# Two token blocks per gate/up chain in a fused state-space and int4 feed-forward kernel

## The chip, the cores and the metric

The kernel runs on one core of a Trainium2 chip. The metric is the device time of one launch in microseconds (us), as the median of several runs. Engines are named as in the profile: PE multiplies matrices, PEld loads its weights, DVE is the vector engine, ACT the scalar (activation) engine, POOL the general-purpose engine, and SP issues most of the DMA transfers.

## The reference: what is computed

The input x has 32 sequences of 64 heads, each of length 1024. Each head is convolved over its length with a state-space kernel K, the product is cut to the sequence's own length, and a feed-forward network with 4-bit weights follows over the 1024 features. Cut to what matters:

```
dtA = A * exp(log_dt);  P = dtA * arange(1024)
K   = 2 * Re( sum_n C * (exp(dtA) - 1) / A * exp(P) )          # one kernel per head
y   = causal_convolution(u * mask, K) + u * mask * D;  y = y * mask
W   = q * s[group] - (z[group] + 1) * s[group]                 # groups of 128 rows
gate, up = y @ Wg, y @ Wu                                      # 1024 -> 2752
out = x + float16( (gate * sigmoid(gate) * up) @ Wd )          # 2752 -> 1024
```

A token is a pair of head and sequence, so there are 64 x 32 = 2048 tokens.

## The kernel before

**Tokens.** The tokens are cut into four blocks of 512, of 16 heads each. For each block the kernel convolves, then computes gate and up, then the down product, and adds the result to x. The convolution's output is held as the sum of two f16 tensors, `xh` and `xl` (tile `self.x`, two buffers of one block each), so every product with it is two matmuls.

**Convolution.** `group` makes the kernels of four or eight heads (phase tables L344-349 with help of DVE or POOL, factors on DVE, a small matmul `kq` L328) and stores them to a DRAM tensor `kpad`. `toeplitz` (L402-410) reads 512 KB of it per head in such a way that the tile holds the Toeplitz matrix. For the first block most of these matrices go into the tiles that later hold the gate and up weights (`w`); the others go into three buffers `t0`. `conv_head` (L413-448) runs 24 matmuls per head (L430) on the input split into `uh` and `ul`; after two heads DVE masks the sum into `y` (L442), ACT casts it to `xh` (L444), and POOL (DVE for the last pair of the first block) subtracts to get `xl` (L446). Matrices are asked for up to four heads ahead.

**Weights.** `unpack` (L454-478) turns 128 x 512 words of 4-bit values into fp8 on DVE: two splits (L466, L467) and eight additions of the zero points (L474). The result goes to a DRAM tensor `m` and is read back in the right layout (L485). Ten such chunks make gate and up, six make the down weights. The loads, stores and reloads are issued by SP, in order with all other SP transfers.

**Chains.** Scales differ per group of 128 rows. Instead of scaling the weights, a chain multiplies its accumulator in PSUM after each group by the ratio of two scales. `gu_chain(ct, blk)` (L513-546) makes one tile of 128 of the 5504 gate and up columns for one block: 8 groups, each two matmuls 128x512 (L520, L521) into one PSUM bank and, but for the last, one rescale of 128x512. There are 43 tiles; gate tile i (Silu into `sg`, L528) is followed by up tile i, whose product with `sg` is `v` (DVE, L534), split into `ih` (ACT cast, L535) and `il` (POOL, L244); the 43rd tile is half gate, half up. `dn_chain(nt, blk)` (L549-568) makes one of eight output tiles: 21 groups of two matmuls (L555, L556) and a rescale, a last matmul (L560), a scaled copy `o` (ACT, L566), the addition to x (L567) and the store.

**Order.** `rescale` (L505-511) gives each rescale to DVE (L508) or ACT (L511) by a running balance, `lag`, of assumed nanoseconds. `roll` (L578-613) interleaves up to six chains (four in the last down stage), one step of each in turn, and advances side work by rates: unpacking and, during the first block's chains, the kernels of heads 16 to 31 and the second convolution; during block 1's, the kernels of heads 32 to 63 and the third convolution; during block 2's, the fourth. Only the first convolution stands ahead of the first chains, with a few unpacking steps between its matmuls. A scheduler then orders each engine's instructions with these as priorities. PSUM has eight banks: six for chains (`ps_ch`), two for convolutions and kernel products (`ps_cv`).

Of the kernel before, what the change touches and what calls it, by code (L numbers as in the profile page):

```python
# [9 lines left out]
F32 = mybir.dt.float32  # L10
# [20 lines left out]
UNPACK_RATE, CONV1_RATE = 0.25, 0.4  # L31
GU_SIDE_RATES, DN_SIDE_RATE = {1: 0.2, 2: 0.15}, 1.0
CHAIN_LEAD = 1.34
# [182 lines left out]
class Core:  # L216
    def __init__(self, ctx, tc, io):
# [8 lines left out]
        self.ps_ch = pool("ps_ch", bufs=6, space=PSUM)  # L226
        self.ps_cv = pool("ps_cv", bufs=2, space=PSUM)
# [4 lines left out]
        self.sg, self.t0, self.us = {}, {}, {}  # L232
# [5 lines left out]
        self.ih = keep.tile([128, 21, 512], F16, name="ih")  # L238
        self.il = keep.tile([128, 21, 512], F16, name="il")
        self.ic = keep.tile([128, 512], F16, name="ic")  # L240
# [11 lines left out]
    def scratch(self, tiles):  # L252
        spaces = [[t.rearrange("p g t -> p (g t)"), 0] for t in tiles]

        def take(shape, dt, name=None):
            n = 1
            for d in shape[1:]:
                n *= d
            size = n * SIZE[dt] // 2
            for sp in spaces:  # L260
                if sp[1] + size <= sp[0].shape[1]:
                    v = sp[0][:shape[0], sp[1]:sp[1] + size].bitcast(dt)
                    sp[1] += size
                    if len(shape) == 3:
                        v = v.rearrange("p (a b) -> p a b", b=shape[2])
                    return v
            raise ValueError(name)

        return take
# [52 lines left out]
    def make_kernel(self, pool, e1, e2, h0, nh):  # L322
        nc = self.nc
        bank = dict(pool=self.ps_ch, tag="ch") if h0 < 16 else dict(pool=self.ps_cv, tag="cv")
        q = bank["pool"].tile([32, 8, 32], F32, name="kq", tag=bank["tag"])[:, :nh, :]
# [7 lines left out]
        for k in range(2):  # L333
            nc.sync.dma_start(self.kpad[h0:h0 + nh, k, 128:].rearrange("h (a b) -> a h b", b=32), kb[:, k])
# [8 lines left out]
    def group(self, pool, h0, nh, xd, tables=None):  # L343
        nc, co = self.nc, self.co  # L344
        side = nc.vector if h0 < 16 else nc.gpsimd
        self.taps(pool, h0)
        with self.after({16: ("y", 4), 24: ("y", 7)}.get(h0)):
            s1, s2, sq_op = phase_tables(nc, side, tables or pool, co, self.cst, h0, nh)
        self.mark(f"sq{h0}", sq_op)
        self.dve(2000)  # L350
# [3 lines left out]
        self.dve(1000)  # L354
# [5 lines left out]
    def groups(self, pool, starts):  # L360
        if len(starts) == 4:
            steps = decay_tables_wide(self.nc, pool, self.co, self.cst, starts[0], 32)
            next(steps)
            for _ in range(4):
                yield
            with self.after("act"):
                xds = next(steps)
        else:
            with self.after("sq8"):
                xds = [decay_tables(self.nc, pool, self.co, self.cst, h0) for h0 in starts]  # L370
# [5 lines left out]
    def conv_fetch(self, h0):  # L376
        src = self.io["xF"][:, h0:h0 + 4, :].rearrange("(c p) h b -> p c h b", p=128)
        cut = lambda d: self.take([128, 8, 4 * B], d).rearrange("p c (h b) -> p c h b", b=B)
        u, uh, ul = cut(F32), cut(F16), cut(F16)
        self.nc.sync.dma_start(u, src)  # L380
        return u, uh, ul

    def conv_split(self, u, uh, ul):
        with self.after("sq4"):
            self.nc.scalar.copy(uh, u)
        with self.after(("e", 4)):
            self.nc.vector.tensor_tensor(ul, u, uh, ALU.subtract)
        return uh, ul
# [13 lines left out]
    def toeplitz(self, h):  # L402
        if h < 8 or 11 <= h < 16:
            j = h if h < 8 else h - 9
# [8 lines left out]
    def conv_head(self, hh):  # L413
        nc = self.nc
        h = hh % 16
        for k in (hh, hh + 1):
            if k // 4 not in self.us and k // 16 == hh // 16:
                self.us[k // 4] = self.conv_load(4 * (k // 4))
        for k in range(hh, hh + (5 if hh < 16 else 3)):
            if k not in self.t0 and k // 16 == hh // 16 and k in self.known:  # L420
# [3 lines left out]
        if h % 2 == 0:  # L424
            bank, tag = (self.ps_ch, "ch") if hh < 16 else (self.ps_cv, "cv")
            self.cq = bank.tile([128, 8, 2, B], F32, name="cq", tag=tag)
        q = self.cq
# [8 lines left out]
        if h % 2 == 1:  # L436
            ts = slice(32 * (h - 1), 32 * (h + 1))
            y = self.ys.pop(0) if hh < 16 else self.cv.tile([128, 8, 2, B], F32, name="y", bufs=1)
            yv = y.rearrange("p g h b -> p g (h b)")
            xh, xl = self.x[hh // 16 % 2]  # L440
            with self.tc.high_priority(offset=100), nullcontext():
                self.mark(("y", hh // 2), nc.vector.tensor_tensor(  # L442
                    y, q, self.mask.unsqueeze(2).to_broadcast([128, 8, 2, B]), ALU.mult))
                nc.scalar.copy(xh[:, :, ts], yv)  # L444
                split = nc.vector if hh == 15 else nc.gpsimd
# [8 lines left out]
    def unpack(self, src, zsrc, dst, rows, w):  # L454
# [7 lines left out]
        a = up.tile([128, 2, 512], I32, name="upk_a")[:rows, :, :w]  # L462
# [42 lines left out]
    def rescale(self, q, col):  # L505
        if self.lag <= 0:
            self.dve(660)
            self.nc.vector.tensor_scalar(q, q, col, None, ALU.mult)  # L508
        else:
            self.act(580)  # L510
            self.mark("act", self.nc.scalar.activation(q, q, AF.Copy, scale=col))  # L511

    def gu_chain(self, ct, blk):  # L513
        nc = self.nc
        q = self.ps_ch.tile([128, 512], F32, name="chq", tag="ch")
        xh, xl = self.x[blk % 2]
        cols = slice(128 * (ct % 21 % 4), 128 * (ct % 21 % 4) + 128)
        for g in range(GH):
            lw = self.wmix[:, g] if ct == 42 else self.wgu[ct // 21][ct % 21 // 4][:, g, cols]
            nc.tensor.matmul(q, lw, xh[:, g, :], start=(g == 0), stop=False, skip_group_check=True)  # L520
            nc.tensor.matmul(q, lw, xl[:, g, :], start=False, stop=(g == GH - 1), skip_group_check=True)  # L521
            if g < GH - 1:
                self.rescale(q, self.rgu[:, ct, g:g + 1])
                yield
        last = self.lgu[:, ct:ct + 1]
        if ct < 21:
            sg = self.fw.tile([128, 512], F32, name="sg", tag="sg", bufs=3)
            nc.scalar.activation(sg, q, AF.Silu, scale=last)  # L528
            self.act(580)
            self.sg[ct] = sg  # L530
        elif ct < 42:
            i = ct - 21
            v = self.fw.tile([128, 512], F32, name="v", bufs=2)
            nc.vector.scalar_tensor_tensor(v, q, last, self.sg.pop(i), ALU.mult, ALU.mult)  # L534
            nc.scalar.copy(self.ih[:, i, :], v)  # L535
            self.dve(660)
            self.act(520)
            self.pool_first(self.il[:, i, :], v, self.ih[:, i, :], ALU.subtract)
        else:
            sg = self.fw.tile([128, 512], F32, name="sg", tag="sg", bufs=3)  # L540
            v = self.fw.tile([128, 512], F32, name="v", bufs=2)
            a, b = slice(0, 64), slice(64, 128)
            nc.scalar.activation(sg[b], q[a], AF.Silu, scale=last[a])
            nc.vector.scalar_tensor_tensor(v[b], q[b], last[b], sg[b], ALU.mult, ALU.mult)
            nc.scalar.copy(self.ic[b], v[b])
            nc.vector.tensor_tensor(self.ic[a], v[b], self.ic[b], ALU.subtract)
        yield

    def dn_chain(self, nt, blk):  # L549
        nc = self.nc  # L550
        q = self.ps_ch.tile([128, 512], F32, name="chq", tag="ch")
        for g in range(GI):
            lw = self.wd[g // 8][nt // 4][:, g % 8, 128 * (nt % 4):128 * (nt % 4) + 128]
            if g < 21:
                nc.tensor.matmul(q, lw, self.ih[:, g, :], start=(g == 0), stop=False, skip_group_check=True)  # L555
                nc.tensor.matmul(q, lw, self.il[:, g, :], start=False, stop=False, skip_group_check=True)  # L556
                self.rescale(q, self.rdn[:, nt, g:g + 1])
                yield
            else:
                nc.tensor.matmul(q, lw, self.ic, start=False, stop=True, skip_group_check=True)  # L560
        rows, cols = slice(128 * nt, 128 * nt + 128), slice(512 * blk, 512 * blk + 512)
# [218 lines left out]
```

## Time and profile before

| What | Value |
|---|---|
| median of 3 runs | 1089.41 us (1087.74 to 1090.03) |
| profiled execution, own time | 1086.84 us |
| its span on the core | 1085.1 us |
| granted PE clock | 0.991 |
| PE, PEld busy | 1024.5, 513.5 us |
| DVE, ACT busy | 905.2, 831.9 us |
| POOL busy | 224.3 us |
| DMA moved | 82.28 MB |

The profile is of one execution, and its span leaves out what lies before the first and after the last instruction. Busy time of an engine includes overlapping instructions only once; a mean duration of one instruction may include overlap with the next. In rows of windows the columns are the window, its length and PE, PEld, DVE, ACT, POOL with busy time and number of instructions, then the granted clock, the DMA share and GB/s. In rows of groups the last part says how long the engine was idle ahead of them and what ended it; rows of waits give the total, the number and the longest.

### The profile page before, as it was taken

The numbers are of one execution on the slowest core, as the hardware profiler recorded it, in microseconds if no ns is written. First come the engines' busy times: TensorE is split into PE (matmuls) and PEld (weight loads), VectorE is DVE, ScalarE is ACT, GpSimd is POOL, SyncE is SP. The second block draws the span as 40 slices with busy tenths as digits, with TensorE's granted clock in tenths as the row PEclk, the third lists the DMA queues.
The fourth block names the chain that finished last, engine by engine and source line by source line (L and its number), as shares of the span: only waits on it lengthen the run. The fifth ranks groups of instructions, "written<-read, shape, count | busy, mean of one in ns | idle before, by whom it ended". The sixth has DMA issues, their size and how long they took to land.

```text
span 1085.1 us, 15582 instructions
## 1 busy us (share of the span) xinstructions
PE 1024.5 (94%) x5834; PEld 513.5 (47%) x5834; DVE 905.2 (83%) x1458; ACT 831.9 (77%) x1371; POOL 224.3 (21%) x178
## 2 busy tenths in 40 slices
PE   2877988899999999999999999999999999999997
PEld 2743444455344445444564444444564444444443
DVE  8989999977998898777768778787768888887887
ACT  5337978877788997777768777777768888888876
POOL 0312234231502121121223012131212111111000
PEclk9899999999999999999999999999999999999999
DMA  5963666530102030110343010011321000000011
GB/s 139 295 222 117 214 188 188 156 123 7 49 1 88 11 92 20 35 44 20 131 132 127 11 49 21 21 56 61 127 79 67 31 30 1 1 1 1 1 40 39
DMA packets 78389, 82.28 MB, mean 76 GB/s; under 512 B 16902, under 2 KB 49798, under 8 KB 78314
## 3 DMA queue, kind: packets, MB, share of 16 engines
q1 hardware_dynamic: 78314, 81.30, 23.4%
q8 instruction: 45, 0.74, 0.3%
q14 instruction: 30, 0.25, 0.1%
HBM read 64.15 MB, written 17.14 MB: 75 GB/s over the span
## 4 chain that ended last, share of the span: by engine, by line
PE 80%; DVE 11%; ACT 3%; DMA 3%; issue 2%; POOL 1%; SPq 0%; DVEq 0%; ACTq 0%; POOLq 0%
PE chq L520 24%; PE chq L521 23%; PE chq L555 13%; PE chq L556 13%; PE cq L430 6%; DVE upk_m L474 3%; DVE chq L508 2%; ACT chq L511 2%; DMA m<-upk_m 1%; DVE v L534 1%; PE chq L560 1%; DMA w<-kpad 1%; PE kq L328 1%; DMA t<-kpad 0%; POOL il L244 0%
## 5 line engine op out<-in xcount | busy, mean ns | idle before, releaser
L520 PE MATMUL chq<-xh,w 128*128 128x512 f16 x1344 | 505.3, 379 | 15.9 <-DVE chq L508 8.2
L511 ACT ACTIVATE chq<-chq,gur 128x512 f32<-128x512 f32 x678 | 431.5, 666 | 98.7 <-PE chq L521 90.6
L521 PE MATMUL chq<-xl,w 128*128 128x512 f16 x1344 | 504.2, 379 | 0.0
L508 DVE TENSOR_SCALAR chq<-chq,gur 128x512 f32<-128x512 f32 x526 | 391.6, 755 | 79.9 <-PE chq L521 58.0
L508 DVE TENSOR_SCALAR chq<-chq,dnr 128x512 f32<-128x512 f32 x321 | 238.6, 755 | 61.5 <-PE chq L556 50.1
L511 ACT ACTIVATE chq<-chq,dnr 128x512 f32<-128x512 f32 x351 | 228.1, 661 | 73.0 <-PE chq L556 68.4
L555 PE MATMUL chq<-ih,wd 128*128 128x512 f16 x672 | 253.0, 379 | 3.0 <-DVE chq L508 1.7
L556 PE MATMUL chq<-il,wd 128*128 128x512 f16 x672 | 253.1, 379 | 0.0
L521 PEld LDWEIGHTS <-w 128*128 128x128 fp8e4 x1344 | 131.2, 98 | 158.4 <-issue 30.5
L244 POOL TENSOR_TENSOR il<-v,ih 128x512 f16<-128x512 f32 x84 | 105.9, 1261 | 461.3 <-ACT ih L535 461.3
L520 PEld LDWEIGHTS <-w 128*128 128x128 fp8e4 x1344 | 131.1, 98 | 135.3 <-issue 2.8
L430 PEld LDWEIGHTS <-t 128*128 128x128 f16 x1224 | 103.0, 98 | 95.5 <-issue 4.0
L430 PE MATMUL cq<-uh,t 128*128 128x256 f16 (+7 forms) x768 | 134.6, 226 | 1.2 <-DMA t<-kpad 1.2
L474 DVE TENSOR_TENSOR upk_m<-upk_a,upk_z 128x512 fp8e4<-128x512 uint8 (+2 forms) x144 | 100.3, 738 | 1.0 <-DMA m<-upk_m 1.0
L556 PEld LDWEIGHTS <-wd 128*128 128x128 fp8e4 x672 | 65.6, 98 | 64.7 <-issue 6.3
L555 PEld LDWEIGHTS <-wd 128*128 128x128 fp8e4 x672 | 65.6, 98 | 61.1 <-issue 1.6
L430 PE MATMUL cq<-ul,t 128*128 128x256 f16 (+7 forms) x384 | 86.3, 225 | 3.5 <-POOL ul L244 3.5
L534 DVE SCALAR_TENSOR_TENSOR v<-chq,gul,sg 128x512 f32<-128x512 f32 x84 | 62.6, 746 | 21.9 <-ACT sg L528 11.6
L528 ACT ACTIVATE sg<-chq,gul 128x512 f32<-128x512 f32 x84 | 57.8, 688 | 11.1 <-PE chq L521 10.3
L535 ACT CAST ih<-v 128x512 f16<-128x512 f32 x84 | 51.6, 614 | 14.6 <-DVE v L534 14.5
L446 POOL TENSOR_TENSOR xl<-y,xh 128x512 f16<-128x512 f32 x24 | 30.3, 1262 | 103.3 <-ACT xh L444 86.0
L567 POOL TENSOR_TENSOR xr<-xr,o 128x512 f32<-128x512 f32 x24 | 28.2, 1177 | 85.8 <-ACT o L566 72.8
(177 smaller groups left out, 448.4 us busy)
## 6 DMA issues: line engine op xcount, KB each, us to landing
t<-kpad SPq DMA_DIRECT2D x51, 512.0 KB, 3.5
w<-kpad SPq DMA_DIRECT2D x13, 512.0 KB, 6.4
u<-xF SPq DMA_DIRECT2D x12, 512.0 KB, 4.1
xr<-xT SPq DMA_DIRECT2D x24, 256.0 KB, 3.5
out<-xr SPq DMA_DIRECT2D x24, 256.0 KB, 2.3
m<-upk_m SPq DMA_DIRECT2D x10, 512.0 KB, 4.4
w<-m SPq DMA_DIRECT2D x10, 512.0 KB, 4.2
upk_p<-qgu SPq DMA_DIRECT2D x10, 256.0 KB, 6.4
```

The lines of the kernel that those rows point to most:

```text
L244: self.nc.gpsimd.tensor_tensor(out, a, b, op)
L430: nc.tensor.matmul(q[:, d:, h % 2, :], t0[:, lw, 128 * d:128 * d + 128], uu[:, 0:8 - d, h % 4, :], start=(d == 0 and k == 0 and h % 2 == 0 ...
L474: nc.vector.tensor_tensor(out, q, minus, ALU.add, saturate=False)
L508: self.nc.vector.tensor_scalar(q, q, col, None, ALU.mult)
L511: self.mark("act", self.nc.scalar.activation(q, q, AF.Copy, scale=col))
L520: nc.tensor.matmul(q, lw, xh[:, g, :], start=(g == 0), stop=False, skip_group_check=True)
L521: nc.tensor.matmul(q, lw, xl[:, g, :], start=False, stop=(g == GH - 1), skip_group_check=True)
L528: nc.scalar.activation(sg, q, AF.Silu, scale=last)
L534: nc.vector.scalar_tensor_tensor(v, q, last, self.sg.pop(i), ALU.mult, ALU.mult)
L535: nc.scalar.copy(self.ih[:, i, :], v)
L555: nc.tensor.matmul(q, lw, self.ih[:, g, :], start=(g == 0), stop=False, skip_group_check=True)
L556: nc.tensor.matmul(q, lw, self.il[:, g, :], start=False, stop=False, skip_group_check=True)
```

## The change

`gu_chain(ct)` now makes one tile for two token blocks at once. Its accumulator has two PSUM banks; per group there are four matmuls, and one rescale of 128x1024 covers both banks. `sg` and `v` are 1024 wide. The products of the first block stay in `ihl` (which replaces `ih` and `il`); those of the second go through a tile `spill` to DRAM and are read back into `ihl` step by step while the last down chain of the first block runs. `dn_chain(n0, blk)` holds two output tiles in two banks, with rescales of 128x512 as before, and stores 512 KB at once.

There are six stages: gate/up of blocks 0 and 1; down 0; down 1; gate/up of blocks 2 and 3; down 2; down 3. Four chains run at once (three in the first two down stages). Convolutions 0 and 1 both stand ahead of the first chains, with the kernels of heads 8 to 31, unpacking and scale ratios at set places between their matmuls; all their matrices use the weight tiles and three `t0` buffers in turn, and are asked for eight heads ahead. Kernels of heads 32 to 63 and convolutions 2 and 3 run beside the two first down stages. One POOL step of the kernel tables of heads 16 to 31 moves to DVE, the kernel stores of heads 0 to 7 move to ACT's DMA queue, the unpacking scratch `upk_a` has one buffer instead of two, and `y` has two instead of one. All PSUM tiles come from one pool of four two-bank buffers.

```diff
-UNPACK_RATE, CONV1_RATE = 0.25, 0.4
-GU_SIDE_RATES, DN_SIDE_RATE = {1: 0.2, 2: 0.15}, 1.0
-CHAIN_LEAD = 1.34
+UNPACK_RATE, LATE_RATE = 0.3, 1.8
+CHAIN_LEAD = 2.0
...
-        self.ps_ch = pool("ps_ch", bufs=6, space=PSUM)
-        self.ps_cv = pool("ps_cv", bufs=2, space=PSUM)
+        self.ps = pool("ps", bufs=4, space=PSUM)
...
+        self.ihl = keep.tile([128, 21, 2, 512], F16, name="ihl")
+        self.ic = [keep.tile([128, 512], F16, name=f"ic{b}") for b in range(2)]
+        self.spill = self.dram.tile([21, 128, 2, 512], F16, name="spill")
+
+    def psum(self, name):
+        return self.ps.tile([128, 2, 512], F32, name=name, tag="ch")
...
-            nc.sync.dma_start(self.kpad[h0:h0 + nh, k, 128:].rearrange("h (a b) -> a h b", b=32), kb[:, k])
+            (nc.scalar if h0 < 8 else nc.sync).dma_start(
+                self.kpad[h0:h0 + nh, k, 128:].rearrange("h (a b) -> a h b", b=32), kb[:, k])
...
-        side = nc.vector if h0 < 16 else nc.gpsimd
+        side = nc.vector if h0 < 32 else nc.gpsimd
...
-        if h < 8 or 11 <= h < 16:
-            j = h if h < 8 else h - 9
+        j = h % 11
+        if h < 32 and j < 8:
...
-        for k in range(hh, hh + (5 if hh < 16 else 3)):
-            if k not in self.t0 and k // 16 == hh // 16 and k in self.known:
+        for k in range(hh, hh + (9 if hh < 32 else 3)):
+            if k not in self.t0 and k // 32 == hh // 32 and k in self.known:
...
-    def rescale(self, q, col):
+    def rescale(self, q, col, n=1):
         if self.lag <= 0:
-            self.dve(660)
+            self.dve(130 + 535 * n)
             self.nc.vector.tensor_scalar(q, q, col, None, ALU.mult)
         else:
-            self.act(580)
+            self.act(220 + 370 * n)
             self.mark("act", self.nc.scalar.activation(q, q, AF.Copy, scale=col))
...
-            nc.tensor.matmul(q, lw, xh[:, g, :], start=(g == 0), stop=False, skip_group_check=True)
-            nc.tensor.matmul(q, lw, xl[:, g, :], start=False, stop=(g == GH - 1), skip_group_check=True)
+            for b, (xh, xl) in enumerate(self.x):
+                nc.tensor.matmul(q[:, b], lw, xh[:, g, :], start=(g == 0), stop=False, skip_group_check=True)
+                nc.tensor.matmul(q[:, b], lw, xl[:, g, :], start=False, stop=(g == GH - 1), skip_group_check=True)
             if g < GH - 1:
-                self.rescale(q, self.rgu[:, ct, g:g + 1])
+                self.rescale(q, self.rgu[:, ct, g:g + 1], 2)
                 yield
...
+            v = self.fw.tile([128, 2, 512], F32, name="v", bufs=1)
+            spill = self.fw.tile([128, 2, 512], F16, name="spill", bufs=1)
             nc.vector.scalar_tensor_tensor(v, q, last, self.sg.pop(i), ALU.mult, ALU.mult)
+            self.dve(1200)
+            for b, hl in enumerate((self.ihl[:, i], spill)):
+                nc.scalar.copy(hl[:, 0], v[:, b])
+                self.act(520)
+                self.pool_first(hl[:, 1], v[:, b], hl[:, 0], ALU.subtract)
+            nc.sync.dma_start(self.spill[i], spill)
...
+            for k in range(2):
+                nt = n0 + k
+                lw = self.wd[g // 8][nt // 4][:, g % 8, 128 * (nt % 4):128 * (nt % 4) + 128]
+                if g < 21:
+                    nc.tensor.matmul(q[:, k], lw, self.ihl[:, g, 0], start=(g == 0), stop=False, skip_group_check=True)
+                    nc.tensor.matmul(q[:, k], lw, self.ihl[:, g, 1], start=False, stop=False, skip_group_check=True)
+                    self.rescale(q[:, k], self.rdn[:, nt, g:g + 1])
+                else:
+                    nc.tensor.matmul(q[:, k], lw, self.ic[blk % 2], start=False, stop=True, skip_group_check=True)
             if g < 21:
+                if n0 == 6 and blk % 2 == 0:
+                    nc.sync.dma_start(self.ihl[:, g], self.spill[g])
                 yield
...
-    events = {"U": lambda: next(unpack_it, None), "R": ratios_gu, "D": ratios_dn}
-    for i, _ in enumerate(c.conv(0)):
-        for e in ("" if i % 8 else "UR" if i == 56 else "UD" if i == 120 else "U"):
-            events[e]()
+    events = {
+        7: [lambda: next(g16)],
+        15: [lambda: next(g8), both(lambda k: c.conv_split(k, 8), 2, 3), lambda: next(g16), lambda: next(g24)],
+        31: [lambda: next(g24)],
+        47: [lambda: next(g16), both(c.conv_fetch, 4, 5)],
+        71: [both(lambda k: c.conv_split(k, None), 4)],
+        79: [lambda: next(g24)],
+        87: [both(c.conv_fetch, 6, 7)],
+        103: [both(lambda k: c.conv_split(k, None), 5)],
+        128: [ratios_gu],
+        159: [both(lambda k: c.conv_split(k, None), 6)],
+        191: [both(lambda k: c.conv_split(k, None), 7)],
+        200: [ratios_dn],
+    }
+    def first_convs():
+        for blk in range(2):
+            yield from c.conv(blk)
+    for i, _ in enumerate(first_convs()):
+        for e in events.get(i, ()):
+            e()
+        if i % 8 == 0 and (32 < i < 120 or i > 190):
+            unpack()
...
+            yield from c.groups(kg2, ScratchPool(take), (32, 40, 48, 56))
+        for blk in (2, 3):
+            yield from c.conv(blk)
...
+    sides = {0: [(unpack_it, UNPACK_RATE)], 1: [(late_it, LATE_RATE)], 2: [(late_it, LATE_RATE)], 4: [(residuals(), 1.0)]}
+    for s in (0, 3):
+        items += [(s, c.gu_chain(ct)) for ct in order]
+        for k in (1, 2):
+            items += [(s + k, c.dn_chain(n0, 2 * (s // 3) + k - 1)) for n0 in (0, 2, 4, 6)]
+    c.lag = 0.0
+    roll(items, lambda stage: {0: 4, 1: 3, 2: 3, 3: 4, 4: 4, 5: 4}[stage], sides, CHAIN_LEAD)
```

## The prediction

> **What bounds the kernel now.** I read the busy totals first, then the page's slices, then the costliest groups, then the stages as windows.
>
> ```profile
> PE 1024.5 (94%) x5834; PEld 513.5 (47%) x5834; DVE 905.2 (83%) x1458; ACT 831.9 (77%) x1371; POOL 224.3 (21%) x178
> ...
> PE   2877988899999999999999999999999999999997
> PEld 2743444455344445444564444444564444444443
> DVE  8989999977998898777768778787768888887887
> ACT  5337978877788997777768777777768888888876
> ```
>
> TensorE (PE) is busy nearly throughout from the ninth slice, about 215 us. In the first eight slices it isn't, and there DVE shows nines. A busy PE may still be late, so I use the lag: the start of an instruction minus the matmul work ahead of it in PE's order. That work is 4128 chain matmuls of 213.7 ns (117 in 25 us) = 882 us, plus 64 convolution heads of some 1.55 us and kernel tables: 987 us. Lag grows only where PE waits. It is 73.5 us at 214 us, 83.2 at the end of the second gate/up stage (520 us), 89.9 at 1005 us and 92.6 at the last matmul; 987 + 92.6 + a tail of 5.5 = the span, 1085.1. So 73.5 of 92.6 us are lost in the first fifth, and only there can much be won.
>
> ```profile
> L511 ACT ACTIVATE chq<-chq,gur 128x512 f32<-128x512 f32 x678 | 431.5, 666 | 98.7 <-PE chq L521 90.6
> L508 DVE TENSOR_SCALAR chq<-chq,gur 128x512 f32<-128x512 f32 x526 | 391.6, 755 | 79.9 <-PE chq L521 58.0
> L474 DVE TENSOR_TENSOR upk_m<-upk_a,upk_z 128x512 fp8e4<-128x512 uint8 (+2 forms) x144 | 100.3, 738 | 1.0 <-DMA m<-upk_m 1.0
> L534 DVE SCALAR_TENSOR_TENSOR v<-chq,gul,sg 128x512 f32<-128x512 f32 x84 | 62.6, 746 | 21.9 <-ACT sg L528 11.6
> ```
>
> Rescales are 823 us of gate/up work on two engines, mean 666 and 755 ns; unpacking is DVE's alone.
>
> ```profile
> 25.00:50.00 25.00, 20.11 (x280) 18.97 (x280) 23.37 (x44) 10.71 (x33) 9.63 (x4) 0.86 0.95 308
> 50.00:75.00 25.00, 16.15 (x143) 12.10 (x144) 21.11 (x35) 5.02 (x9) 6.64 (x4) 0.86 0.72 245
> ...
> 125.00:150.00 25.00, 21.65 (x129) 10.75 (x128) 25.00 (x47) 20.66 (x36) 9.73 (x4) 1.00 0.57 186
> ...
> 225.00:250.00 25.00, 25.00 (x161) 13.22 (x160) 19.43 (x27) 18.27 (x30) 6.71 (x5) 1.00 0.23 76
> ...
> 500.00:525.00 25.00, 25.00 (x144) 12.69 (x143) 20.61 (x29) 20.00 (x33) 4.58 (x4) 1.00 0.17 53
> ```
>
> (PE, PEld, DVE, ACT, POOL; clock; DMA share; GB/s.) From 125 to 200 us DVE is full: it sets the pace. From 225 PE is, and DVE and ACT have 5 us of slack in 25. From 50 to 75, in the first convolution, ACT is nearly idle and PE waits for its kernel matrices:
>
> ```profile
> PE cq L430 <- DMA w<-kpad: 8.4, 4, 2.5
> ```
>
> **The change, part by part.** The matmuls and PE's 987 us stay. What moves is lag.
>
> *Merged rescales.* 1204 of 128x512 become 602 of 128x1024. No row has that form. DVE's tensor ops on 128x256 and 128x512 take 416 and 680 ns, so 512 more columns cost some 530 ns; ACT's cast of 128x1024 takes 1.03 us against 0.614, so 415. By the rows: 755 + 530 = 1.29 us (DVE), 666 + 415 = 1.08 (ACT), and a merge saves 225 or 251 ns. [...] On a full engine I take 1.19 us (DVE) and 1.0 (ACT). [...]
>
> *Two convolutions ahead.* The first begins at some 29 us. 32 heads of 1.6 us are 51 us, so 80 at best. SP's queue goes in order: each unpacked weight chunk puts a zero-point load, a store and a reload between the matrix loads, and each waits for DVE. I place those waits at about 54, 62 and 74 us, from DVE's order and 6.5 us per chunk; the matrix loads for heads 15, 19 and 23 are queued behind. Before, four such waits cost PE 8.4 us in 16 heads. I take 12 us for 32 heads (ends 5 and 22): convolutions end at 92 us (85 to 102). The DMA rings say the same: 32 matrices, four more u loads and three chunks (1.3 MB each) are 22.8 MB from 27 us on; at the 308 GB/s of the 25 to 50 us row, whose DMA share is 0.95, 74 us, at 400 GB/s 57: 84 to 101. Tables of groups 16 and 24, formerly beside chains, now go here; their POOL products (2.084 us each) go to DVE (0.682): eight, under 6 us, within this sum. Their four kernel stores join SP's queue at some 0.5 us each, in front of matrix loads; those of groups 0 and 4 leave it for ACT's, idle there. Before, gate/up began at 70.75; it now begins 22 us later, but with 16 heads (26 us of PE) done.
>
> *Gate/up stage 0.* A pair (gate and up tile, two blocks) is 64 matmuls = 13.65 us of PE, 14 rescales, two long ACT reads (Silu 1.1, casts 1.2), one product of 1.2 us and 14 unpack operations until unpacking ends. DVE: 14 x 0.789 = 11 us with the splits, plus 1.2 for v, plus two or three rescales = 14.2 to 15.3; ACT: eleven or twelve rescales and 2.3 us = 13 to 14. So DVE still sets the pace for eight pairs: first product at 122 us (DVE must finish queued unpacking), then seven times 15 = 228 us. The PE work ahead of that point is 170 us: lag 58 instead of 73.5. The gain is 15.5 us. [...] Pairs 9 to 21 need 12 to 13 us of ACT in 13.65: tight with four chains in flight, where before it was six of half the size. A chain has 3 x 0.855 = 2.56 us for its rescale (before 5 x 0.43 = 2.14), but two queued merged ones take 2.0 to 2.4, where three small ones took 2.0. I add 3 (0 to 8).
>
> *Stages 1 and 2.* Before, tables of groups 32 to 56 and the third convolution ran beside 95 us of gate/up work and cost some 8 us of the lag between 214 and 520. Their scratch is the first x buffer, free now only after stage 0, and at a side rate of 1.8 they bunch: some 46 us of DVE work, rescales included, in 35 to 38 us of PE. I take 13 (8 to 18). Twenty heads drain at the end of stage 2 with matrix loads of 3.5 us and one u buffer: +3.
>
> *Products through DRAM.* 42 stores and 42 reloads of 256 KB. Nearest rows: out<-xr, 256 KB, 2.3 us; xr<-xT 3.5. A reload is issued when the last chain of block 0 passes a step, and the next block wants it two rounds of three chains later, 2 x 3 x 0.855 = 5.1 us. Cost zero, hidden behind those chains' matmuls. If SP stands behind an output store whose residual add is late, the cover goes and PE loses about 3 us once; without cover on each of 42 steps it would be 1 us each.
>
> *Rest.* Stages 3 to 5 have what before had from 520 on, 9 us; there DVE and ACT sink to some 9 us per 13.65, which costs and gains nothing, as PE is already full. A two-bank last chain adds 2 us to the lag, and the final stores of 512 KB instead of 256 add 1 to the tail. One more activation table load: 1.28, in the head, hidden beside matrix waits. Output adds stay off the path.
>
> Sum: lag 58 + 3 + 13 + 3 + 9 + 2 = 88; 987 + 88 + 6.5 = 1081.5 as span, against 1085.1. Median minus span was 4.3 (the profiled execution itself took 1.74 more than its span), so about 1086 if all is carried over; but DVE and ACT are emptier in stage 3 where the old run lost 2 to 4 of those 9, so I take 3 off: 1083.
>
> **Rivals.**
>
> *Slower: stage 1's bunch.* If DVE's tables and rescales there run one behind another (each table step waits for PE, ACT or POOL and holds DVE's order), loss is not 13 but 30 to 35: 1100 to 1105. For it: in the head the same tables leave PE waiting 19.3 us for e1t. Against: the three chains go on while tables wait. It decides from a loss of about 19 us.
>
> *More gain.* SP's waits cost only 5 us, convolutions end at 85, first product at 112, and ACT takes twelve rescales a pair at 1.0: lag 45 to 48 at the eighth product, some 1068. For it: matrix loads are prefetched nine ahead. Against: DVE is full in all rows to 200 us, and neither frees it.
>
> *No change.* Two-block chains only shift the pace from DVE to ACT (1.08 rather than 1.0 is 1 us per pair); the 15 us shrink to 9, and 1087 to 1091 results.
>
> **How the numbers follow.** Likeliest case 0.42 (1083, own range 1076 to 1091), more gain 0.17, slower 0.32, no change 0.09. 0.2% (2.2 us) is about what this kernel's runs can tell from nothing. Faster (under 1087.2): 0.29 + 0.16 + 0.01 = 0.46. Within: 0.07 + 0.06 = 0.13; slower 0.41. For 8 in 10, 1062 to 1108.
>
> **What would show it.** Merged rescales: 1.2 to 1.3 us (DVE), 1.0 to 1.1 (ACT). Convolution heads end near 92 us, with waits for w<-kpad around heads 15 to 23. The eighth product near 228. In stage 1, PE waits on DVE rescales and tables near 13 us. Waits of PE for reloaded products: none. I am wrong if PE is full from 110 us on, if stage 1 loses over 19, or if a merged ACT rescale is over 1.15 us.

## The result and the profile after

The changed kernel takes 1153.74 us (four runs, 1151.39 to 1156.15) against 1088.79 before (four runs, among them the three known at the prediction): 1.0596 times the time, 95% interval 1.0571 to 1.0622. 1083 was forecast. The profiled execution took 1156.15 us, its span is 1154.4, so the profile shows one 2.4 us slower than the median.

The page's busy totals and slices of the changed kernel:

```profile
PE 1060.4 (92%) x5834; PEld 517.5 (45%) x5834; DVE 832.6 (72%) x1138; ACT 767.2 (66%) x1003; POOL 205.9 (18%) x175
...
PE   3578899899999997899998999999999999999995
DVE  8697999973677688766663367667667767777775
ACT  5511788789777766656763367777776776777774
PEclk9798999999999997999999999999999999999998
```

Both vector engines have less to do (832.6 and 767.2 us where it was 905.2 and 831.9), as forecast, and the span is longer all the same. PE's row has dents where the one before had little but its head: besides the head, the slices from 433 to 490 us, the one from 606 us, and a deeper one at the very end. The clock row dips in the head, in the slice from 433 us and at the end.

The costliest groups, by shape, and last the small rescales on ACT in the kernel before:

```profile
L518 ACT ACTIVATE chq<-chq,gur 128x1024 f32<-128x1024 f32 x349 | 370.6, 1087 | 127.6 <-PE chq L528 125.5 <-DVE chq L515 1.4
L515 DVE TENSOR_SCALAR chq<-chq,gur 128x1024 f32<-128x1024 f32 x253 | 324.9, 1290 | 134.9 <-PE chq L528 130.7 <-ACT chq L518 2.5 <-ACT sg L535 0.8
L515 DVE TENSOR_SCALAR chq<-chq,dnr 128x512 f32<-128x512 f32 x320 | 232.0, 755 | 101.6 <-PE chq L569 90.6 <-ACT chq L518 4.1 <-PE cq L438 1.1
L518 ACT ACTIVATE chq<-chq,dnr 128x512 f32<-128x512 f32 x352 | 224.1, 663 | 121.7 <-PE chq L569 101.6 <-DVE chq L515 15.6 <-PE cq L438 2.8
```

```profile
L511 ACT ACTIVATE chq<-chq,dnr 128x512 f32<-128x512 f32 x351 | 228.1, 661 | 73.0 <-PE chq L556 68.4 <-PE cq L430 0.7
```

Merged rescales take 1.087 and 1.290 us by their mean; from start to start on a full engine they hold ACT 1.01 and DVE 1.20 us (medians over the trace), where two small ones hold 1.16 and 1.32. The price was right. New are the idle reasons of the changed kernel's last row: down-stage rescales on ACT (`dnr`) now wait 15.6 us for DVE's, where the row before names PE alone.

By stage:

```profile
25.00:50.00 25.00, 13.62 (x177) 11.77 (x178) 15.43 (x27) 15.39 (x38) 5.46 (x3) 0.84 0.96 268
50.00:75.00 25.00, 18.33 (x247) 16.79 (x245) 24.53 (x42) 5.91 (x12) 9.28 (x6) 0.82 0.78 238
75.00:100.00 25.00, 18.34 (x221) 16.91 (x218) 25.00 (x44) 3.67 (x6) 7.58 (x6) 0.80 0.92 297
100.00:125.00 25.00, 21.05 (x223) 15.20 (x222) 16.55 (x24) 7.14 (x10) 9.21 (x6) 0.93 0.73 242
...
425.00:450.00 25.00, 20.45 (x71) 7.03 (x68) 21.46 (x52) 14.48 (x23) 10.38 (x17) 0.82 0.16 54
450.00:475.00 25.00, 19.26 (x102) 7.24 (x100) 22.93 (x57) 20.36 (x36) 4.09 (x3) 0.84 0.22 66
...
625.00:650.00 25.00, 22.16 (x278) 18.95 (x279) 5.71 (x9) 6.05 (x10) 10.33 (x7) 0.93 0.88 288
...
1125.00:1150.00 25.00, 16.89 (x59) 5.58 (x57) 14.79 (x22) 12.72 (x21) 0.00 (x0) 0.89 0.17 63
```

In the head ACT does 5.9, 3.7 and 7.1 us of work in 25, while DVE is full from 50 to 100 us (24.53 and 25.00) and PE's granted clock is 0.80 to 0.84. In the first down stage (425 to 475) PE is short by over 10 us in 50 at a clock of 0.82 and 0.84; at 625 to 650 convolution heads run with hardly any vector work beside them; and the last window shows a stage that runs dry.

What PE waits for (the rows that matter here):

```profile
PE kq L329 <- DVE e1t L203: 20.9, 2, 14.3
PE cq L438 <- DVE y L450: 12.6, 7, 3.7
PE chq L568 <- DVE chq L515: 11.5, 12, 2.3
PE chq L527 <- DVE chq L515: 9.5, 15, 1.8
PE cq L438 <- DMA w<-kpad: 7.6, 3, 2.9
PE cq L438 <- DMA t<-kpad: 5.2, 4, 3.0
PE chq L568 <- DMA ihl<-spill: 1.2, 3, 0.5
```

Convolution matmuls that wait for DVE's mask `y` are new: before, this pair is not among the waits at all. The wait for the kernel factors `e1t` is old (19.3 us before). Reloaded products cost 1.2 us.

The lag was followed at five points of the work. Counted from both traces with the same lengths, PE's work is 980 us, 7 less than the prediction's count, so the forecast's span of 1081.5 us would give a sum of 101.5 on this count instead of 94.5.

| Up to the point | forecast | changed kernel | unmerged kernel (below) |
|---|---|---|---|
| start of down 0, 340 us of work | 61 | 85.7 | 79.3 |
| down 0, with its kernel tables, to 387 | +13 | +26.9 | +14.1 |
| down 1 and the convolutions left over, to 537 | +3 | +25.8 | +22.7 |
| second gate/up stage, to 829 | | +7.5 | +3.4 |
| down 2 and 3, to 968 | +11 for these two rows | +11.4 | +2.1 |
| the end | +6.5 | +17.0 | +10.3 |
| sum | 94.5 | 174.3 | 131.9 |

Before, the lag at 340 us of work was 83.8, and at the end 105.

### The profile page after: what moved, and what is told of

The parts are those of the page before. It is cut to its first block, busy times and chain, and to the rows that moved or that the text cites. A ratio compares the mean times of both kernels' runs of the same rounds, so it can differ in the third digit from the quotient of the medians.

```text
span 1154.4 us, 16008 instructions
## 1 busy us (share of the span) xinstructions
PE 1060.4 (92%) x5834; PEld 517.5 (45%) x5834; DVE 832.6 (72%) x1138; ACT 767.2 (66%) x1003; POOL 205.9 (18%) x175
## 4 chain that ended last, share of the span: by engine, by line
PE 72%; DVE 15%; ACT 4%; DMA 4%; issue 4%; SPq 1%; POOL 0%; DVEq 0%; ACTq 0%
PE chq L527 22%; PE chq L528 22%; PE chq L568 12%; PE chq L569 10%; PE cq L438 5%; DVE chq L515 5%; DVE upk_m L481 5%; ACT chq L518 3%; DMA ihl<-xF 1%; DMA t<-kpad 1%; DMA ihl<-spill 1%; DVE y L450 1%; ACT o L582 1%; DVE v L542 1%; DMA kpad<-kb 1%
## 5 line engine op out<-in xcount | busy, mean ns | idle before, releaser
L527 PE MATMUL chq<-xh,w 128*128 128x512 f16 x1344 | 507.2, 380 | 14.6 <-DVE chq L515 8.2
L518 ACT ACTIVATE chq<-chq,gur 128x1024 f32<-128x1024 f32 x349 | 370.6, 1087 | 127.6 <-PE chq L528 125.5
L515 DVE TENSOR_SCALAR chq<-chq,gur 128x1024 f32<-128x1024 f32 x253 | 324.9, 1290 | 134.9 <-PE chq L528 130.7
L568 PE MATMUL chq<-ihl,wd 128*128 128x512 f16 x672 | 243.8, 383 | 21.0 <-DVE chq L515 11.5
L569 PE MATMUL chq<-ihl,wd 128*128 128x512 f16 x672 | 242.1, 385 | 0.0
L245 POOL TENSOR_TENSOR ihl<-v,ihl 128x512 f16<-128x512 f32 x42 | 52.7, 1255 | 504.0 <-ACT ihl L545 504.0
L438 PEld LDWEIGHTS <-t 128*128 128x128 f16 x960 | 67.8, 99 | 27.7 <-DMA t<-kpad 6.8
L438 PE MATMUL cq<-uh,t 128*128 128x256 f16 (+7 forms) x592 | 70.6, 230 | 5.5 <-DMA t<-kpad 5.2
L542 DVE SCALAR_TENSOR_TENSOR v<-chq,gul,sg 128x1024 f32<-128x1024 f32 x42 | 53.8, 1280 | 19.9 <-PE chq L528 19.3
L451 ACT CAST xh<-y 128x512 f16<-128x512 f32 x32 | 19.7, 615 | 69.1 <-DVE y L450 69.0
L438 PE MATMUL cq<-ul,t 128*128 128x256 f16 (+7 forms) x296 | 58.6, 230 | 0.0
L535 ACT ACTIVATE sg<-chq,gul 128x1024 f32<-128x1024 f32 x42 | 46.8, 1115 | 11.2 <-PE chq L528 10.7
```

The source lines that it names most:

```text
L245: self.nc.gpsimd.tensor_tensor(out, a, b, op)
L438: nc.tensor.matmul(q[:, d:, h % 2, :], t0[:, lw, 128 * d:128 * d + 128], uu[:, 0:8 - d, h % 4, :], start=(d == 0 and k == 0 and h % 2 == 0 ...
L527: nc.tensor.matmul(q[:, b], lw, xh[:, g, :], start=(g == 0), stop=False, skip_group_check=True)
L568: nc.tensor.matmul(q[:, k], lw, self.ihl[:, g, 0], start=(g == 0), stop=False, skip_group_check=True)
L569: nc.tensor.matmul(q[:, k], lw, self.ihl[:, g, 1], start=False, stop=False, skip_group_check=True)
```

## The experiments

Theory A, formed on the trace: the program orders the two banks of one PSUM tile as one object. Then a rescale of one half holds the other half's matmuls and rescale, and the two chains of a tile run in turn rather than side by side. Theory B is the prediction's own slower rival: the kernel tables of heads 32 to 63 bunch on DVE in down 0. Theory C: products come back late from DRAM. Where no number of runs is given, a time is of one run; the four runs of the changed kernel lie within 4.8 us, and the kernel before took 1085.5 to 1090.3 us beside these experiments.

The end of the changed kernel shows what A means. PE, and DVE below it, in the last 14 us:

```profile
1140.73 0.38 PE L568 MATMUL chq<-ihl,wd 128*128 128x512 f16 x1
1142.25 0.38 PE L568 MATMUL chq<-ihl,wd 128*128 128x512 f16 x1 [0.92 <-DVE chq L515]
1144.11 0.43 PE L568 MATMUL chq<-ihl,wd 128*128 128x512 f16 x1 [1.27 <-DVE chq L515]
1145.82 0.58 PE L568 MATMUL chq<-ihl,wd 128*128 128x512 f16 x1 [0.85 <-DVE chq L515]
```

```profile
1141.44 0.76 DVE L515 TENSOR_SCALAR chq<-chq,dnr 128x512 f32<-128x512 f32 x1 [2.10 <-PE chq L569]
1143.31 0.75 DVE L515 TENSOR_SCALAR chq<-chq,dnr 128x512 f32<-128x512 f32 x1
1145.00 0.76 DVE L515 TENSOR_SCALAR chq<-chq,dnr 128x512 f32<-128x512 f32 x1 [0.95 <-PE chq L569]
```

These four pairs of matmuls alternate between the two banks of one tile. Each starts only when the rescale of the pair before it, in the other bank, has ended: 1141.44 + 0.76 = 1142.20, next matmul 1142.25; 1143.31 + 0.75 = 1144.06, next 1144.11. The program's own order says the same without any time. Rescales in down stages that the built program makes wait for a semaphore of DVE or ACT, and not for PE alone:

```
kernel before      25 of 672
changed kernel    624 of 672
```

A two-bank tile is also freed only as a whole, but that costs little here: PE waits 0.5 us in all for the read-out `o` of a finished chain.

**Control with drained edges.** The test of A needs one-bank tiles in the down stages and two-bank tiles in gate/up stages, so the pool is closed and opened between them: the last chain of one kind ends before the first of the other begins, a drained edge. This is the control, with no other difference.

```diff
+    def banks(self, n):
+        if hasattr(self, "ps_stack"):
+            self.ps_stack.close()
+        self.ps_stack = self.ctx.enter_context(ExitStack())
+        self.nb = n
+        self.ps = self.ps_stack.enter_context(self.tc.tile_pool(name=f"ps{n}", bufs=8 // n, space=PSUM))
...
-        return items and len(active) < width(items[0][0])
+        return items and len(active) < width(items[0][0]) and not (
+            active and (items[0][0] % 3 == 0) != (active[0][0] % 3 == 0))
```

> A control: the changed kernel, with its PSUM pool closed and opened again where a gate/up stage meets a down stage, so that chains of the two kinds no longer overlap there; tiles stay two banks wide. All theories: 0 to 8 us slower than the changed kernel's 1153.7 us, for the drained edges.

It took 1187.67 us: 34 more, not 0 to 8. The same with one-bank tiles in the down stages, for the chains and for the late convolutions' pairs of heads:

```diff
-        q = self.psum("chq")
+        halves = [self.psum("chq")[:, 0] for _ in range(2)]
         for g in range(GI):
             for k in range(2):
+                q = halves[k]
...
+         lambda stage: c.banks(2 if stage % 3 == 0 else 1))
```

> As the control, but in the down stages the pool holds eight one-bank tiles: a down chain's two output tiles, and the late convolutions' pairs of heads, lie in tiles of their own. Theory A (the two banks of one tile are ordered as one object, so that a rescale of one half holds the matmuls of the other): 25 to 45 us faster than the control, about 1115, with hardly a down-stage rescale that waits for another rescale. Theory B (DVE's bunch of kernel tables in the first down stage makes the loss): under 8 us faster. Theory C (reloads of products from DRAM are late): no change.

It took 1155.74 us, 32 less than its control; the first half of theory A's forecast held, but a control that is off by 34 us needs to be understood first. In it all chains of a stage start in one round. So both were run again with chains two rounds apart after each edge (`clock - since >= lead * len(active)`, with `since` set at the edge).

> The control again, but after each drained edge the chains start two rounds apart, as they do at the start of the changed kernel (in the first control they all started in one round and then finished together). If the bunched starts made the first control's 34 us: about 1157 to 1165. If the drained edges themselves did: still above 1175.

> As the second control, but with one-bank tiles in the down stages (and for the late convolutions). Theory A (the two banks of one tile are ordered as one object): 25 to 40 us faster than the second control. If the 32 us between the first pair came of their bunched starts instead: under 10 us faster.

The second control took 1188.78 us, so the starts were not the cause: a drained edge itself is dear. The one-bank version took 1137.08 us, 51.7 less. That is more than forecast, and its waiting rescales fell to 22 of 672. The waits that theory A names go with the tile's width, which is worth 32 and 52 us in the two pairs. Between 450 and 650 us the lag grows by 41 us in the control, by 18 with one-bank tiles; from 1000 us to the end by 38 and 11. This fits a turn that nothing fills where few chains are left, as at a drained edge and at the end; why a drained edge costs the control 34 us was not taken further apart.

**One-bank tiles in the head alone.** Each pair of heads of convolutions 0 and 1 has its own tile, the rest is as in the first control.

> As the control, but one-bank tiles in the head alone: each pair of heads of the first two convolutions has its own tile. Theory A: the 12.4 us in which the head's matmuls wait for the masking on DVE go, the convolutions end 10 to 12 us sooner (98 to 100 us), and the whole gains 3 to 10 us on the control, since unpacking on DVE then sets the pace. A rival, that DVE alone sets the end of the head: nothing gained.

1186.45 us, 1.2 less than its control, which one run each can't tell from nothing. PE's waits in the head, of the changed kernel and of this one:

```profile
PE cq L438 <- DVE y L450: 12.4, 6, 3.7
PE cq L438 <- DMA w<-kpad: 7.6, 3, 2.9
PE kq L329 <- DVE e1t L203: 6.6, 1, 6.6
```

```profile
PE kq L336 <- DVE e1t L203: 12.2, 1, 12.2
PE cq L445 <- DMA w<-kpad: 8.4, 6, 3.9
PE cq L445 <- DMA t<-kpad: 4.4, 1, 4.4
```

The 12.4 us for `y` (14.2 in the control) are gone and come back as waits for the kernel factors `e1t` (6.6 to 12.2; 6.9 in the control) and for matrices (7.6 to 12.8; 5.6 in the control). The last convolution matmul starts at 113.1 us, in the control at 114.8. So the shared tile is real in the head, and worth nearly nothing there. Its forecast of 98 to 100 us was wrong. The rival that the expectation named fits: DVE does 24.98 and 25.00 us of work from 50 to 100 us here too. Work was not taken off DVE to test it.

**ACT's order in the head.** In the changed kernel ACT stands before the cast of an input chunk whose load is late, with the sines of group 8 behind it, and DVE waits for these. ACT's row and DVE's:

```profile
40.03 1.04 ACT L390 CAST uh<-ihl 128x1024 f16<-128x1024 f32 x1 [5.38 <-DMA ihl<-xF]
41.09 1.28 ACT L188 ACT_TABLE_LOAD   x1
42.38 0.94 ACT L188 ACTIVATE r<-r 128x512 f32<-128x512 f32 x2
```

```profile
43.87 0.43 DVE L199 SCALAR_TENSOR_TENSOR e2t<-r,xd 128x256 f32<-128x256 f32 x1 [8.01 <-ACT r L190]
```

```diff
-        71: [both(lambda k: c.conv_split(k, None), 4)],
+        71: [both(lambda k: c.conv_split(k, 16), 4)],
```

(and the same for chunk 5).

> The changed kernel; only the casts of input chunks 4 and 5 on ACT in the head are put behind the phase tables of group 16, so that ACT doesn't stand before the sines of group 8 waiting for a load. If DVE sets the end of the head: its 8.0 us of waiting for ACT go, the convolutions end 6 to 8 us sooner (102 to 104), and the whole gains 5 to 8 us. If the shared tiles' waits set it: under 2 us.

1151.93 us, 1.8 less than the median of the changed kernel and inside its four runs. In the trace the 8.0 us shrink to 2.2, the convolutions end at 110.4 us (102 to 104 expected), and the lag at 250 us is 78.8 for 82.4. The mechanism is there at about half its forecast size. PE's waits in the head fall from 26.6 to 20.9 us: those for `e1t` from 6.6 to 1.8 and for matrices from 7.6 to 3.4, while those for masks stay (12.6) and 3.1 for a copy on ACT are new.

**Without the late kernel tables.** Heads 32 to 63 take the kernels of heads 0 to 31.

```diff
-            yield from head_coefficients(nc, nc.gpsimd, co, take, c.prm, c.cst[:, 66:67], 32, 32)
-            yield from c.groups(kg2, ScratchPool(take), (32, 40, 48, 56))
+            c.known.update(range(32, 64))
+            yield
...
-            t0, bass.AP(self.kpad.tensor, self.kpad.offset + h * 2304 + 1, ap=[[1, 128], [1152, 2], [1, L]])
+            t0, bass.AP(self.kpad.tensor, self.kpad.offset + h % 32 * 2304 + 1, ap=[[1, 128], [1152, 2], [1, L]])
```

> The changed kernel without the kernel tables of heads 32 to 63: left out are their coefficients, tables, kernels and stores, and convolutions 2 and 3 use the kernels of heads 0 to 31. Theory B (the tables' bunch on DVE): 22 to 30 us faster than 1153.7. Theory A (shared tiles): 8 to 14 us faster, because the chains stay serialized without the tables.

> The kernel of the previous run, without the kernel tables of heads 32 to 63 (left out; convolutions 2 and 3 use the kernels of heads 0 to 31). If the tables' 21 us came of DVE's bunch itself, they are saved here too: 17 to 23 us faster than with them. If they came of chains that the shared tiles left without slack: under 10.

> The kernel before without the kernel tables of heads 32 to 63 (left out; convolutions 2 and 3 use the kernels of heads 0 to 31). If the place of the tables, beside three chains of a down stage, makes their 21 to 25 us in the changed kernel: 3 to 10 us faster than before, since there they run beside 95 us of gate/up work. If the tables cost what they cost wherever they are: 20 us or more.

The changed kernel without them took 1132.70 us, 21.0 less, just under theory B's 22 to 30. The one-bank version without them took 1111.95, 25.1 less. The kernel before without them took 1078.91, 9.5 less than its 1088.43. So the tables cost some 21 to 25 us, whatever the tiles, and some 12 to 15 us of that come of the new place: the tables cost 9.5 us beside gate/up chains and more than twice that beside three down chains. The windows without them, in the changed kernel:

```profile
425.00:450.00 25.00, 24.30 (x138) 11.61 (x137) 15.83 (x20) 17.88 (x27) 2.27 (x2) 1.00 0.23 75
450.00:475.00 25.00, 24.69 (x182) 14.18 (x181) 15.55 (x23) 15.19 (x24) 5.06 (x4) 1.00 0.38 124
```

Against the two windows shown of the full kernel, DVE drops from 21.46 and 22.93 us to 15.83 and 15.55, and the clock stays at 1.00.

**Without the round trip through DRAM.** `dma_start` of `spill`, both ways, is left out.

> The changed kernel without its stores and reloads of products through DRAM (the second block of each pair uses the first block's products; 42 stores and 42 reloads are left out). Theory C (reloads late): 5 us or more faster. Theory A: within 3 us of 1153.7.

1151.96 us, 1.8 less than the median and inside the runs' spread: theory C falls.

**The merge undone.** All tiles one bank wide, in one pool of eight, no drained edges; two token blocks are still taken at once.

```diff
-        self.ps = pool("ps", bufs=4, space=PSUM)
+        self.ps = pool("ps", bufs=8, space=PSUM)
...
-        q = self.psum("chq")
+        halves = [self.psum("chq")[:, 0] for _ in range(2)]
...
             for b, (xh, xl) in enumerate(self.x):
+                q = halves[b]
...
+                if g < GH - 1:
+                    self.rescale(q, self.rgu[:, ct, g:g + 1])
             if g < GH - 1:
-                self.rescale(q, self.rgu[:, ct, g:g + 1], 2)
                 yield
```

> The merge undone, the rest kept: one pool of eight one-bank tiles for everything; a gate/up chain still takes two token blocks, but in two tiles with two rescales of 128x512, and a down chain's two outputs, and each pair of convolution heads, have their own tiles. No drained edges. Theory A (shared tiles cost 40 us or more, the merge itself saves little): 1105 to 1125. If merged rescales are worth more than the shared tiles cost: 1150 or more, with a lag at the end of the first gate/up stage some 15 us worse.

1113.83 us: 39.9 less than the changed kernel, with all 1204 small rescales back. 31 of 672 down rescales wait for another. The table above has its lag by stage: it gains in each one, 6.4 us by the start of down 0, 12.8 in down 0, 3.1 in down 1, 4.1 in the second gate/up stage, 9.3 and 6.7 in the last two rows; the sum, 42.4, is the difference of the two spans. Of it 31.9 us lie in down 0 to 3 and the end, where the two kernels' rescales have the same size and only the tiles differ, and there is no drained edge. Even in the gate/up stage, which the merge was to relieve, the merged kernel is behind.

**Late side work at other rates.**

```diff
-UNPACK_RATE, LATE_RATE = 0.3, 1.8
+UNPACK_RATE, LATE_RATE = 0.3, 2.8
```

> The previous kernel with the late side work at a rate of 0.9 instead of 1.8 per chain step, so that the kernel tables of heads 32 to 63 spread over twice as many steps of the down stages. If their bunching on DVE is the loss: the first down stage loses 8 to 12 us less, part of which comes back as convolution heads left to the end of the second: 3 to 8 us faster. If the amount of work alone counts: the same.

> The unmerged kernel with the late side work at a rate of 2.8 instead of 1.8 per chain step. In it PE lost some 16 us between 575 and 640 us, where the convolution heads that are left at the end of the second down stage run without chains beside them and wait for their matrices. If the missing chain steps are the cause: that loss goes to 5 us or less, and the whole is 8 to 12 us faster than 1113.8. If SP's loads of the matrices are the cause whatever runs beside them: under 3 us.

On the unmerged kernel 0.9 (the first text above) gives 1114.01 us, no change from 1113.83, where 3 to 8 less were expected. In its trace down 0 loses 2 us less, not 8 to 12, and down 1 loses 3.5 more. So the tables cost more in the new place, but that their bunching is the reason isn't shown. 2.8 gives 1107.46, 6.4 less (8 to 12 expected). The end of down 1, unmerged at rate 1.8 and then at 2.8:

```profile
575.00:600.00 25.00, 19.09 (x225) 15.61 (x223) 8.32 (x12) 8.20 (x14) 13.19 (x10) 0.93 0.76 254
600.00:625.00 25.00, 19.61 (x274) 17.21 (x272) 6.14 (x9) 4.33 (x7) 9.44 (x8) 1.00 0.73 233
```

```profile
575.00:600.00 25.00, 21.46 (x197) 14.02 (x196) 13.74 (x18) 13.48 (x22) 10.08 (x8) 1.00 0.62 205
600.00:625.00 25.00, 21.80 (x237) 16.06 (x234) 10.97 (x16) 9.90 (x16) 7.84 (x6) 1.00 0.45 153
```

At 1.8 both vector engines idle here (ACT 8.20 and 4.33 us of 25) while heads run alone and PE waits for their matrices; at 2.8 chains are still running beside them (13.48 and 9.90). From 575 to 640 us the lag grows by 14.5 us at 1.8 and by 8.2 at 2.8, and PE's waits for the matrices (`t` from `kpad`) go from 11.3 to 6.5. Missing chain steps are thus part of the cause; the 8 us left are more than the 5 expected, and what they come of isn't shown.

**What helps, together.** Unmerged, rate 2.8, and the two casts moved.

> The unmerged kernel at a late rate of 2.8 and with the casts of input chunks 4 and 5 behind the phase tables of group 16: what is found to help, together. If the gains add up: 1099 to 1106, still slower than before; the tables (21 to 25 us) and the head are what is left.

1104.53 us (four runs, 1103.72 to 1109.08), ratio to before 1.0164, interval 1.0138 to 1.0190. Of the 65 us that the change costs, 49 go with these three steps, taken one on top of another (39.9, 6.4 and 2.9); the first undoes the shared tiles and the merge at once. The tables' new place, 12 to 15 us by the runs above, was not undone on top of them. No complete version that was tried beats the kernel before.

## Why the prediction was wrong

**The step that failed: what a two-bank tile orders.** The part on the rest reads "Stages 3 to 5 have what before had from 520 on", and the part on products has a down chain's next step "two rounds of three chains later, 2 x 3 x 0.855 = 5.1 us". Both count a step's four matmuls as one piece of PE work, with the rescales of its two halves going on side by side. In this program the halves take turns: `dn_chain` with two outputs in one tile is not two of the former chains, it is one chain twice as long. No term was put down for this and no rival had it. Runs that change only the tiles of the down stages show 32 and 52 us with drained edges. Without drained edges it is 40 with the merge undone too, some 32 of them in the down stages and the end.

**Merged rescales.** The cost per instruction was right: 1.20 us on DVE and 1.01 on ACT held, 1.19 and 1.0 taken. No run known at the prediction shows these two terms, for none has a rescale of 128x1024. The trace before gives them only by addition: on a full engine a small rescale holds DVE 0.66 us and ACT 0.58 (medians from start to start between 100 and 520 us), and 0.53 and 0.415 for 512 more columns make 1.19 and 1.0. Against two small ones a merge so saves 0.12 and 0.15 us, not the 0.225 and 0.251 of the means. What was wrong is that the saving reaches the end. The unmerged kernel arrives at down 0 6.4 us earlier, though its convolutions end at the same time (113.8 and 113.9 us), and gains another 4.1 in the second gate/up stage. So freed engine time was not what these chains lacked. That they lacked independence fits, but the run undoes the merge and the shared tiles at once and doesn't tell them apart in these stages. The forecast's sum for DVE per pair comes to 14.6 to 15.8 us by its own terms, not 14.2 to 15.3; the 15 that was used lies in both.

**The head.** Forecast: convolutions end at 92 us, first product at 122, eighth at 228. Measured: 113.9, 142.0 and 250.1. The pace between, 15.4 us a pair, is the 15 forecast, so the whole miss is ahead of the first product. The 12 us that were put down for SP's matrix loads came to 7.6 by name, but 12.4 for masks and 6.6 for `e1t` lay beside them: 26.6 instead of 12. The 400 GB/s of the prediction's transfer estimate is reached in short windows alone (404 and 400 from 40 to 42 and 42 to 44 us before); of the 25 us rows shown for the changed kernel 297 is the most. PE is also slower: from 26 to 114 us its granted clock is 0.84, and matmuls that follow one another without a gap take some 9 us more than the same shapes at 1.00, of which the forecast's 1.6 us a head hold 2. Together that is the 22 us. Experiments that took away the waits for masks or most of those for `e1t` moved the end by 1.8 and 3.5 us: several chains of work finish close together here, DVE's full row among them, and I had summed one. That row was misread as well: "DVE is full in all rows to 200 us" does not hold for the 21.11 us of 50 to 75 us before; with the change DVE is full there. ACT, which the prediction found nearly idle from 50 to 75 us (5.0 us of work), has 5.9 there with the change, and in the whole head it idles more, not less. With both convolutions ahead, ACT has no rescales until 110 us; up to the end of unpacking it idles 102 us in the changed kernel (247.7 us), and 68 in the one before (215.8 us).

**Down 0.** That the tables cost time in this place was right; that they do so by bunching isn't shown. Forecast 13 (8 to 18), measured 26.9, and 14.1 with tiles and merge undone. The slower rival named 30 to 35 as its price and 19 as the point from which it decides, so by the prediction's own sign it held, though its 1100 to 1105 us was passed as well. The tables' own part, 21 to 25 us over the whole kernel, is above my range too.

**Down 1.** "+3" for heads left at the end was too low by far: 25.8 measured, and 22.7 with tiles and merge undone. The price of a drain was taken per matrix load, as if chains ran on beside it; at rate 1.8 they run out first. A rate of 2.8 gets 6.4 us of it back. What else makes up this row was not taken apart.

**Products through DRAM.** Cost zero was right: 1.2 us of waits, and no gain that one run can tell when all 84 transfers are left out.

**The end.** Forecast 2 + 6.5 for a lone two-bank chain and the tail, measured 17.0 in the last row: a lone chain of this kind takes 1.5 to 1.9 us from one half's matmuls to the other's. With one-bank tiles the row is 10.3.

## What to carry to other kernels

Before a wider instruction is priced, look at what its wider tile is ordered against: count, in the built program, the waits of each user of the tile, before and after. Here that count went from 25 to 624 of 672 and could be had before any run. Engine time that is saved on an engine with slack is worth nothing if the same edit makes two independent chains take turns; and if work is moved out of the shadow of other work, ask what the engines that used to fill that time will do in it.

## What the runs showed of the hardware that had not been expected

In a stalled stage PE's granted clock fell to a half, and this made the stall longer. In down 0 PE idles for 1.98 us ahead of a matmul at 440.87 and for 2.34 us ahead of one at 454.49, and then:

```profile
440.00:444.00 4.00, 3.13 (x8) 0.78 (x7) 3.36 (x8) 2.06 (x4) 0.09 (x1) 0.64 0.15 49
444.00:452.00 8.00, 7.18 (x17) 2.13 (x17) 5.78 (x19) 5.19 (x8) 0.00 (x0) 0.54 0.11 41
455.00:461.00 6.00, 5.21 (x13) 1.57 (x11) 5.55 (x13) 3.79 (x7) 0.00 (x0) 0.50 0.00 0
```

At a granted clock of 0.50 the matmuls from 456.40 us on start 0.427 us apart instead of 0.214. If all 38 matmuls of these three windows ran at half clock they cost 8 us more (38 x 0.213), of the 26.9 that the stage loses; with the first window's 0.64 it is somewhat less. Without the tables the windows from 425 to 475 us stay at 1.00, and the kernel before shows 1.00 in every window of 25 us from 100 to 1075 us. The half clock follows each of the two gaps; that a gap brings the clock down, and how long or how frequent gaps would have to be, no run here tells. In the prediction a wait of PE was priced at its own length.

In one place of the changed kernel a short DVE operation beside a long POOL operation took as long as that one. POOL's row, and DVE's:

```profile
45.94 2.12 POOL L245 TENSOR_TENSOR ul<-ihl,uh 128x1024 f16<-128x1024 f32 x1 [0.30 <-ACT uh L390]
```

```profile
46.19 2.16 DVE L202 TENSOR_TENSOR e1t<-e1t,r 128x256 f32<-128x256 f32 x1
56.93 0.41 DVE L202 TENSOR_TENSOR e1t<-e1t,r 128x256 f32<-128x256 f32 x1
```

The same operation, 128x256, takes 0.41 us at 56.93 and 2.16 us at 46.19, where it ends just after POOL's. Which of the two held the other, and by what, no run here tells.
